# Four GNN layers on one core: the end of each batch paced to 117 units instead of 75

## The chip, the cores and the metric

One core of a Trainium2 chip. The time is that of the device for one execution, in microseconds, the median of several runs.

## The reference, cut to what matters

Sixteen graphs of 1024 nodes and 128 features go through four layers. Each layer adds its output to its input. Layers 0 and 1 multiply by the dense adjacency, layer 2 scores every edge with a small network (twice, each time with an update of the nodes), layer 3 is graph attention:

```python
# layer 0, 1: x = x + gnn(relu(layernorm(x)), adj)      (dense adj)
# layer 2, for l in 0, 1:
#   scores = sigmoid(relu(a[:, :, None] + b[:, None]) @ We2[l])   per edge
#   messages = (adjacency * scores) @ x ; x = layernorm(x + mlp([x, messages]))
# layer 3:
e = (Wh1 + swapaxes(Wh2)) * (A + eye); e = where(e >= 0, e, 0.2 * e)
attention = softmax(where(A_ > 0, e, NEG_INF)); h_prime = attention @ Wh
x = x + elu(h_prime)
```

## The kernel before

Only about 1.5% of the adjacency is set, so the kernel turns each block of it into one-hot tiles (`on`, `onT`, `om`, `omT`: the building) and runs the edge scores on the edges alone (the rounds). Three lanes are emitted side by side in each period: the rounds of batch b, the end of batch b-1 (last update and layer 3) and the beginning of batch b+1 (layers 0 and 1, then the building). Each lane yields a number of units a step, and the lane that is least far through its allowance goes next:

```python
MAIN_US, FIRST_US, LAST_US = 243.0, 118.0, 75.0      # allowances
...
        def weave(self, lanes):
            out_of = [[0.0, i, gen, us] for i, (gen, us) in enumerate(lanes)]
            while out_of:
                least = min(out_of, key=lambda v: v[:2])
                us = next(least[2], None)
                if us is None:
                    out_of.remove(least)
                else:
                    least[0] += us / least[3]
```

Emission is a priority, not the final order: when the program is built, the instructions are put in order for each engine, and an instruction that is believed ready can pass another. The strips of layer 3 look like this (cut):

```python
N_ROW = {"m": 2, "a": 2, "c": 1}          # row buffers; strips use "c": one buffer
...
            for lo, hi in L3_ROWS:         # three blocks of 3, 3 and 2 tiles
                for k in range(0, T, 2):   # four strips each: 12 a batch
                    at = strip(k, lo, hi)  # DMA into the one buffer
                    ...                    # e = (wh1 + wh2) * at         VectorE, twice
                    nc.vector.scalar_tensor_tensor(e, e, L3_ALPHA, e, op0=OP.mult, op1=OP.max)
                    nc.scalar.activation(e, e, AF.Exp)
                    nc.vector.scalar_tensor_tensor(e, at, 0.0, e, op0=OP.is_gt, op1=OP.mult)
                    ...                    # matmuls hp; the mask above is the last reader of at
                    yield 1.2 * n
```

## Time and profile before

| | before |
|---|---|
| time | 5532 us |
| a period (mean of 12, from the first `hid` of a batch to that of the next) | 337.1 us |
| of it until the first `rank` of the building (stretch A) / from there on (stretch B) | 189.5 / 147.6 us |
| store of the output, after the period's first `hid` | 309 us |
| VectorE waiting for a strip | 2.0 us a period |
| TensorE clock at half | 2.0 us a period |

A `hid` is an instruction of the rounds and a `rank` one of the building; rows two to four come from the starts of single instructions in the trace.

The other readings of before are in the prediction.

### The profile page before, as it was taken

The page shows a single profiled execution, that of the slowest core. Times are in us where ns is not written, and L with a number is a line of the kernel's source. Part 1 is how long each engine was busy: PE and PEld are TensorE (multiplying, and loading weights), DVE is VectorE, ACT ScalarE, POOL GpSimd, SP SyncE. Part 2 cuts the span into 40 slices and gives each one's busy share as a digit, 9 for nine tenths or more (in the row PEclk, how much of TensorE's full clock was granted, in tenths as well). Part 3 has the DMA queues.
Part 4 walks back from the last instruction along what each step waited for, and adds up shares of the span by engine and source line. Part 5 has one row for each costly group of instructions (what it writes and reads, how often), then busy time and mean ns, then how long its engine had stood idle before and what let it go on. Part 6 is the DMA issues. An engine that isn't in the chain of part 4 may idle for free.

```text
span 5526.6 us, 113576 instructions
## 1 busy us (share of the span) xinstructions
PE 5037.3 (91%) x45109; PEld 3719.3 (67%) x45109; DVE 4304.6 (78%) x10759; ACT 3054.6 (55%) x6790; POOL 184.9 (3%) x137
## 2 busy tenths in 40 slices
PE   5999999999999999999999999999999999999996
PEld 4676766667676666666766666676766767666664
DVE  4777787878879787787877878778787887978886
ACT  4555564655647555465555646556465564655543
POOL 0000000000000000000000000000000000000000
PEclk8999999999999999999999999999999999999998
DMA  6242424243242433424334142432424324243111
GB/s 174 62 136 87 121 68 137 76 125 101 84 140 66 125 96 92 131 66 120 98 102 124 56 139 81 122 106 71 140 72 128 97 85 133 67 124 95 54 63 51
DMA packets 740139, 554.56 MB, mean 100 GB/s; under 512 B 32272, under 2 KB 686352, under 8 KB 739600
## 3 DMA queue, kind: packets, MB, share of 16 engines
q1 hardware_dynamic: 734496, 545.58, 33.6%
q8 instruction: 356, 5.83, 0.4%
q10 hardware_dynamic: 5104, 1.65, 0.1%
q14 instruction: 183, 1.50, 0.1%
HBM read 446.44 MB, written 100.66 MB: 99 GB/s over the span
## 4 chain that ended last, share of the span: by engine, by line
PE 47%; DVE 27%; DMA 9%; ACT 9%; issue 4%; POOL 3%; SPq 0%; ACTq 0%; DVEq 0%; POOLq 0%
PE pre L986 11%; DVE val L1075 10%; PE p L1097 6%; DMA at<-in_adj_dram 4%; DVE hid L1003 4%; PE nb L288 4%; PE msg L1114 4%; PE bb L296 3%; PE sc L1018 3%; DMA a<-adjT 2%; DVE omT L854 2%; PE hp L505 2%; POOL st L243 2%; PE h L342 2%; PE tn L743 2%
## 5 line engine op out<-in xcount | busy, mean ns | idle before, releaser
L1003 DVE SCALAR_TENSOR_TENSOR hid<-pre,hid 128x320 f16<-128x320 f32 (+1 forms) x2048 | 993.0, 504 | 294.9 <-ACT hid L1002 283.9
L1002 ACT ACTIVATE hid<-pre 128x320 f16<-128x320 f32 (+1 forms) x2048 | 900.7, 454 | 501.3 <-PE pre L986 473.4
L986 PEld LDWEIGHTS <-part 128*128 128x128 f16 x8192 | 753.4, 98 | 450.5 <-issue 236.2
L986 PE MATMUL pre<-on,part 128*128 128x320 fp8e4 (+1 forms) x4096 | 966.2, 309 | 71.6 <-DVE hid L1003 60.6
L986 PE MATMUL pre<-om,part 128*128 128x320 fp8e4 (+1 forms) x4096 | 994.3, 309 | 0.0
L1114 PE MATMUL msg<-upd,xf 128*128 128x128 f32 (+3 forms) x3008 | 613.6, 323 | 2.2 <-DVE upd L1105 2.2
L1075 DVE TENSOR_TENSOR val<-onT,u 128x384 f32<-128x384 fp8e4 (+1 forms) x1152 | 607.8, 580 | 4.0
L1097 PE MATMUL p<-val,omT 128*128 128x128 f16 x6528 | 534.2, 219 | 29.8 <-DVE val L1075 27.7
L1097 PEld LDWEIGHTS <-omT 128*128 128x128 fp8e4 x6528 | 436.7, 96 | 84.4 <-DVE val L1075 34.4
L1075 DVE TENSOR_TENSOR val<-omT,u 128x384 f32<-128x384 fp8e4 x896 | 439.2, 549 | 0.0
L861 ACT ACTIVATE om<-pm 128x320 fp8e4<-128x320 f32 (+1 forms) x576 | 268.9, 467 | 294.4 <-PE pm L817 285.8
L1114 PEld LDWEIGHTS msg<-upd,xf 128*128 128x128 f32 x3008 | 414.2, 191 | 25.6 <-DVE upd L1105 13.9
L1105 DVE SCALAR_TENSOR_TENSOR upd<-p,adj 128x512 f32<-128x512 f32 x512 | 348.5, 681 | 82.4 <-PE p L1097 82.2
L1097 PE MATMUL p<-val,onT 128*128 128x128 f16 x4480 | 374.1, 219 | 1.4 <-DVE upd L1105 1.4
L847 ACT ACTIVATE onT<-pn 128x384 fp8e4<-128x384 f32 (+1 forms) x576 | 297.6, 517 | 102.7 <-PE pn L817 82.8
L1039 ACT ACTIVATE srow<-sc,be_s,down 128x128 f32<-128x128 f32 (+2 forms) x512 | 259.7, 540 | 168.2 <-PE sc L1018 166.9
L505 PE MATMUL hp<-wh,e 128*128 128x129 f32 x2048 | 318.3, 285 | 22.3 <-DVE e L502 22.3
L1097 PEld LDWEIGHTS <-onT 128*128 128x128 fp8e4 x4480 | 304.6, 97 | 36.9 <-issue 8.8
L505 PEld LDWEIGHTS hp<-wh,e 128*128 128x128 f32 x2048 | 275.5, 195 | 51.9 <-DVE e L502 29.6
L804 ACT ACTIVATE far<-iota_off,mid 128x384 f16<-128x384 f16 x448 | 269.5, 625 | 39.9 <-DVE on L808 34.3
L288 PE MATMUL nb<-z,ct 128*128 128x128 f32 x2048 | 279.3, 282 | 12.4 <-DMA ct<-in_adj_dram 11.9
L1018 PE MATMUL sc<-hid,slide 128*32 128x320 f16 (+1 forms) x4096 | 268.3, 315 | 18.2 <-DVE hid L1003 15.7
(220 smaller groups left out, 8106.8 us busy)
## 6 DMA issues: line engine op xcount, KB each, us to landing
at<-in_adj_dram SPq DMA_DIRECT2D x128, 512.0 KB, 4.3
ct<-in_adj_dram SPq DMA_DIRECT2D x128, 512.0 KB, 4.6
adjT<-tn SPq DMA_DIRECT2D x128, 512.0 KB, 5.1
l<-adjT SPq DMA_DIRECT2D x128, 512.0 KB, 4.2
adj<-adjT SPq DMA_DIRECT2D x256, 256.0 KB, 3.4
a<-adjT SPq DMA_DIRECT2D x128, 384.0 KB, 3.5
adj<-adjT SPq DMA_DIRECT2D x448, 64.0 KB, 2.1
adj<-adjT SPq DMA_DIRECT2D x192, 128.0 KB, 2.6
```

The costliest lines, as they stand in the source:

```text
L288: nc.tensor.matmul(ps, mat[:, k], z[:, k], start=(k == 0), stop=(k == T - 1))
L505: nc.tensor.matmul(sums[:, t], e[:, i, t * P : (t + 1) * P], wh[:, k + i, : D + 1], start=False, stop=True, skip_group_check=True,)
L804: nc.scalar.activation(far[:, : ck * P], self.iota[t == u][:, : ck * P], AF.Abs, bias=s.mid[:, i : i + 1])
L847: nc.scalar.activation(onT, pn[:, : ck * P], AF.Copy, saturate=False)
L986: nc.tensor.matmul(pre[:, :c], path.parts[node // Q][:, k, node % Q, v], hot[:, :c], start=(hot is on and k == 0), stop=(hot is om and k = ...
L1002: nc.scalar.activation(hid[:, 0, :c], pre[:, :c], AF.Relu)
L1003: nc.vector.scalar_tensor_tensor(hid[:, 1, :c], pre[:, :c], 0.0, hid[:, 0, :c], op0=OP.max, op1=OP.subtract)
L1018: ins = nc.tensor.matmul(self.sc[g * G : (g + 1) * G, : self.c], self.path.slide[:, self.l, G - 1 - r : 2 * G - 1 - r], self.hid[self.done ...
L1075: nc.vector.tensor_tensor(pair[:, i % 2, :ck], right[:, :ck], v.to_broadcast([P, ck, P]), op=OP.mult)
L1097: nc.tensor.matmul(self.ps[d][:, i], left[:, k], halves[:, k, :, h], start=(k, h) == terms[0], stop=(k, h) == terms[-1],)
L1105: nc.vector.scalar_tensor_tensor(upd, self.ps[d], S_SCALE, self.adj[:, d * Q : (d + 1) * Q], op0=OP.add, op1=OP.mult,)
L1114: nc.tensor.matmul(self.msg[h][:, (lo - h * Q) * P : (hi - h * Q) * P], self.xf[mb // Q][:, mb % Q], up, start=False, stop=True, skip_grou ...
```

## The change

Its intent: the building is heavy on VectorE, and the end of the batch before lies partly beside it. With a larger allowance the end counts as less far along at each step, so it is emitted sooner, and is done when the building begins.

```diff
 MORE_DIAG = 0
 
 
+
 MAIN_US = 243.0
 FIRST_US = 118.0
-LAST_US = 75.0
+LAST_US = 117.0
```

The added blank line shifts line numbers by one: L496 of before is L497 after.

## The prediction

> **What bounds the kernel now.** I read the page first, then the kernel's interleaving code, then busy time by stretch of one batch, the groups of instructions inside a stretch, and the waits.
>
> ```profile
> PE 5037.3 (91%) x45109; PEld 3719.3 (67%) x45109; DVE 4304.6 (78%) x10759; ACT 3054.6 (55%) x6790; POOL 184.9 (3%) x137
> ...
> PE 47%; DVE 27%; DMA 9%; ACT 9%; issue 4%; POOL 3%; SPq 0%; ACTq 0%; DVEq 0%; POOLq 0%
> ```
>
> The first line is busy time by engine, the second the chain that ended last. TensorE leads both, but VectorE holds 27% of the chain: an average over stages with different limits. The interleaving code says which stages. In each period three lanes are emitted together, each step going to the lane that is least far through its own allowance: the rounds of batch b (steps add up to about 243.6 units, allowance 243), the end of batch b-1 (last update 20 units, last layer 12 plus 38.4 for twelve strips, 70.4 in all, allowance 75) and the beginning of batch b+1 (70 units of layers 0 and 1, then 46.8 units of building the one-hot tiles, 116.8, allowance 118). So the building starts at 70/118 = 0.59 of the way and lasts to the end; the end of the batch before reaches 70.4/75 = 0.94 and lies beside both.
>
> In the trace, batch starts (the first `hid` of each batch) are 335 to 340 us apart. I take the period 1480 to 1815 us, in which the first `rank` of the building is at 1669. Busy time by stretch: before and during the building, then the last period, which has rounds and end but no beginning of another batch.
>
> ```profile
> 1480.00:1669.00 189.00, 175.68 (x1470) 130.38 (x1469) 137.04 (x373) 93.11 (x203) 9.81 (x7) 1.00 0.45 130
> 1669.00:1815.00 146.00, 135.85 (x1350) 99.82 (x1350) 130.82 (x298) 97.07 (x223) 1.64 (x1) 1.00 0.22 68
> 5184.00:5434.00 250.00, 226.11 (x1897) 154.93 (x1897) 203.96 (x480) 102.51 (x232) 6.10 (x5) 0.98 0.19 57
> 1669.00:1753.00 84.00, 79.53 (x826) 59.89 (x826) 80.65 (x183) 59.29 (x139) 0.00 (x0) 1.00 0.22 66
> ```
>
> Columns: stretch, length, busy PE, PEld, DVE, ACT, POOL, then granted clock and DMA. VectorE is busy 137/189 = 73% in the first stretch (call it A) and 131/146 = 90% in the second (B); in the first 84 us of B it is 80.65/84 = 96%[...]. ScalarE goes from 49% to 66%. TensorE shows 93% in both, but that needs correcting:
>
> ```profile
> 2057.66 0.33 PE L850 MATMUL pq<-rank,on 128*128 128x128 f16 x3
> ...
> 2059.62 0.22 PE L1097 MATMUL p<-val,omT 128*128 128x128 f16 x1
> ```
>
> One matmul of 128 columns shows 0.22 us, three in a row 0.33: each further one costs 0.055, and the rest is a tail that overlaps the next. Giving every matmul the start-to-start time that its own form shows when matmuls run in a row (0.055 us for 128 columns of f16, 0.135 for 320, 0.11 for 128 of f32) TensorE needs 158.6 us in A (84%) and 115.9 in B (79%). So B is held by VectorE and A by TensorE and its bubbles: the building waits there for `omT`, `on`, `onT` in turn.
>
> **What the Trainium skill says.** "Perfetto Trace Analysis", Identifying the Most-Contended Engine: matmul occupancy doesn't measure distance from the limit, occupancy of VectorE and ScalarE does; the two timeline lines above agree. The same page, Optimization Strategy: where the most contended engine changes over time, interleaving the regimes may help. That is what this change attempts: VectorE goes from 73% to 90% between A and B. "PSUM — Partial Sum Buffer", Engine vs sequencer instructions: VectorE and ScalarE queues are strict FIFO. So an instruction of the end that stands ahead of one of the building delays it; the 96% agrees with a queue that rarely runs dry, though no line proves the order.
>
> **The change part by part.** One number, the allowance of the end, goes from 75 to 117 (and a blank line moves all line numbers by one). No instruction is added, removed or resized. With 117 the end reaches 70.4/117 = 0.60 when it is done: just where the building begins (0.59). What moves is that part of the end which lies in B now:
>
> ```profile
> L505 PE MATMUL hp<-wh,e 128*128 128x129 f32 x80 | 12.9, 284 | 0.2 <-DVE e L502 0.2
> ...
> L496 DVE SCALAR_TENSOR_TENSOR e<-whr,whc,a 128x256 f32<-128x256 f32 (+1 forms) x14 | 7.3, 532 | 0.5 <-DMA a<-adjT 0.5
> L502 DVE SCALAR_TENSOR_TENSOR e<-a,e 128x768 f32<-128x768 f32 (+1 forms) x8 | 6.5, 813 | 0.0
> L500 DVE SCALAR_TENSOR_TENSOR e<-e 128x512 f32<-128x512 f32 (+1 forms) x7 | 5.6, 795 | 0.0
> L501 ACT ACTIVATE e<-e 128x512 f32<-128x512 f32 (+1 forms) x7 | 5.1, 726 | 0.0
> L495 DVE TENSOR_TENSOR a<-a,ident 128x128 f32<-128x128 f32 x7 | 1.8, 284 | 0.0
> L513 ACT ACTIVATE o<-hp,rsum 128x128 f32<-128x128 f32 x5 | 1.6, 366 | 0.1
> L425 DVE SCALAR_TENSOR_TENSOR o<-o,neg 128x1024 f32<-128x1024 f32 x1 | 1.2, 1216 | 0.0
> L426 DVE SCALAR_TENSOR_TENSOR xb<-o,xb 128x1024 f32<-128x1024 f32 x1 | 1.2, 1214 | 0.0
> L424 ACT ACTIVATE neg<-neg 128x1024 f32<-128x1024 f32 x1 | 1.1, 1057 | 0.1
> ```
>
> These are groups inside B: count, busy us, mean ns, idle before. VectorE: 7.3 + 6.5 + 5.6 + 1.8 + 1.2 + 1.2 + 0.7 (`neg`) + 0.5 (sums) = 25 us. ScalarE: 5.1 + 1.6 + 1.1 = 8 us. TensorE: 80 matmuls at 0.112 paced = 9 us. After the move:
>
> - B: VectorE 131 - 25 = 106, TensorE 116 - 9 = 107, ScalarE 97 - 8 = 89 us.
> - A: VectorE 137 + 25 = 162, TensorE 159 + 9 = 168, ScalarE 93 + 8 = 101 us.
>
> In B nothing is then near 90% at the old length. How short it gets depends on how well three nearly equal engines overlap. The last period shows what two lanes with equal loads manage: VectorE 204/250 = 82%, TensorE paced 197/250 = 79%. I take 83% for TensorE and VectorE in B, which has the building's independent tiles as filler: 107/0.83 = 129 us, 17 less than 146. In A, TensorE keeps its 84%: 168/0.84 = 200 us, 11 more than 189; VectorE there is then at 162/200 = 81%, as in the last period. I let the end's independent strips fill some of A's bubbles (`hid`, `xf`, the load of `xm`) and count 8 to 9 instead of 11. Net: -17 + 8.5 = -8.5 us for each period that has all three lanes. Those are b = 1 to 14: 14 x -8.5 = -119 us. The first period has no end lane, the last no building (its end just moves forward, 0 ± 3 us), and the drain is unchanged. 5532 - 119 gives about 5413; I put down 5412.
>
> **The rivals.**
>
> 1. *The gain is given back in A.* TensorE's total work is the same; A already waits for chains. If A pays in proportion at a worse packing (168/0.81 = 207 us, +18), the net is about 0 and the time stays at 5530. For it: A's TensorE reaches 84% with VectorE at 73%, and each extra wait for `hid` or `val` there costs both. Against it: in stretches of A TensorE is nearly solid, so A can be packed.
>
> 2. *The strips' loads block the one DMA queue.* All strips go through one row buffer, and the queue waits in order:
>
> ```profile
> SPq L1190 <- DVE e L502: 579.7, 108, 38.1
> SPq L689 <- PE tn L743: 792.9, 107, 26.1
> ```
>
> This is SyncE's own waiting in the whole run: 580 us for a strip's buffer, 38 at most. In the change twelve strips must pass in about (0.60 - 0.27) x 335 = 110 us, one each 9 us, where a cycle of load (3.3 us median from issue to landing), three VectorE passes, Exp and the release takes 8 us unhindered (3.3 + 0.6 + 1.2 + 0.9 + 0.8 + 0.9). Loads of `at`, `ct` and the rounds' rows wait behind it, in the very stretch whose DMA share is 0.45. Then A grows by some 20 us and the kernel is about 1% slower, 5570. Against it: the end runs late rather than blocks if other work is placed ahead of a strip that isn't ready.
>
> 3. *B packs as its start does now.* If VectorE and TensorE reach 90% in B (119 us, -27) and A pays 6, the net is -21 a period, 5240. For it: VectorE's 96% now. Against it: equal loads on three engines hinder one another more than one full engine does.
>
> 4. *The order on the engines isn't the emission order.* Of the last layer's strips, 7 of 12 lie in B, by work 53%, where the units say 67%: the order is adjusted when the program is built, so some of the move has happened already. I counted from the trace, so it's in the sum, but a reordering can undo part of the rest.
>
> **Range and chances.** Rival 1 and the central case are the nearest, 3 and 2 the ends. Half-way to 3 gives 5300, part of 2 gives 5520. I expect it to hold 5300 to 5510 eight times in ten. The line for 2% faster is 5532.2 x 0.98 = 5421.6, just above my centre: 0.53 for faster, 0.43 within, 0.04 slower.
>
> **What would show it.** In the changed profile the period should be 326 to 331 us. The output's store, now 307 to 312 us after the batch's first `hid`, should come at about 200 to 220. VectorE in the building stretch should fall from 90% to 80 to 85% and that stretch to about 129 us; the stretch before should grow to about 198 us with VectorE over 80%. The waits of TensorE for `omT` should shrink. The prediction is wrong if the building stretch stays near 146 us with VectorE idle (then chains bound it, not VectorE), if the stretch before grows by 15 us or more, or if waits for strips or `at` loads grow by several us a period.

## More of the kernel before

Every run of the kernel before lay between 5515 and 5543 us.

The waits, from the list of who waited for whom (total us, times, longest):

```profile
DVE e L496 <- DMA a<-adjT: 31.9, 37, 3.1
DVE a L495 <- DMA a<-adjT: 4.3, 4, 2.5
```

So VectorE waits hardly at all for strips: 36 us in the whole run.

## The result, and the profile after

The changed kernel took 5735 us (5728 to 5736, four runs) against 5534 in the same sessions. The ratio is 1.036, with a 95% interval of 1.034 to 1.038: 3.6% slower, where 2.2% faster was predicted and 5510 was the upper end of the range. Ratios here are the mean time of one kernel's fast runs over that of the other's of the same rounds, so not quite the ratio of the medians quoted.

The page of the changed kernel, busy time by engine and the chain that ended last:

```profile
PE 5137.8 (90%) x45109; PEld 3783.2 (66%) x45109; DVE 4323.8 (75%) x10759; ACT 3072.7 (54%) x6790; POOL 176.8 (3%) x137
...
PE 41%; DVE 34%; DMA 10%; ACT 8%; POOL 3%; issue 3%; SPq 0%; ACTq 0%; DVEq 0%; POOLq 0%
```

The counts are the same to the instruction, VectorE's work hardly grew (4305 to 4324 us), and yet its share of the chain rose from 27 to 34%: it now holds others up more often. TensorE's busy time rose by 100 us for the same matmuls.

A period grew from 337.1 to 351.0 us (mean of 12). Busy time by stretch of one period, then the last period:

```profile
1527.00:1735.00 208.00, 187.92 (x1542) 141.00 (x1541) 153.94 (x404) 98.03 (x211) 9.31 (x7) 0.98 0.44 130
1735.00:1878.00 143.00, 129.76 (x1284) 93.15 (x1283) 115.57 (x267) 93.20 (x215) 1.64 (x1) 0.99 0.18 53
5379.00:5641.00 262.00, 226.50 (x1878) 154.29 (x1877) 204.70 (x479) 103.77 (x231) 5.66 (x5) 0.97 0.18 54
```

The columns are those of the prediction: stretch, length, PE, PEld, DVE, ACT, POOL, clock, DMA. Stretch A grew from 189 to 208 us, B shrank from 146 to 143, and the last period grew from 250 to 262. In A VectorE has 17 us more work but a share of 74% only (153.94/208): the time isn't VectorE's work. The clock column went from 1.00, 1.00 and 0.98 to 0.98, 0.99 and 0.97.

Who waits for strips now (the same view as in the section on before):

```profile
DVE e L497 <- DMA a<-adjT: 84.3, 43, 3.7
DVE a L496 <- DMA a<-adjT: 61.2, 45, 3.3
```

That makes 145 us of VectorE standing still, 36 before; over the twelve periods 9.5 us each against 2.0. VectorE in order of time, in one period (start, length, engine, line, operation, tiles, count, and in brackets the idle time before it and its releaser), then SyncE's queue in the same stretch:

```profile
2722.22 0.95 DVE L503 SCALAR_TENSOR_TENSOR e<-a,e 128x768 f32<-128x768 f32 x1
...
2727.53 0.62 DVE L497 SCALAR_TENSOR_TENSOR e<-whr,whc,a 128x384 f32<-128x384 f32 x1 [3.50 <-DMA a<-adjT]
...
2730.91 0.96 DVE L503 SCALAR_TENSOR_TENSOR e<-a,e 128x768 f32<-128x768 f32 x1 [0.91 <-ACT e L502]
2731.78 0.34 DVE L330 SCALAR_TENSOR_TENSOR o<-nb,deg,b_bc 128x128 f32<-128x128 f32 x1
2732.04 1.21 DVE L1004 SCALAR_TENSOR_TENSOR hid<-pre,hid 128x480 f16<-128x480 f32 x2
2735.97 0.49 DVE L496 TENSOR_TENSOR a<-a,ident 128x128 f32<-128x128 f32 x2 [2.72 <-DMA a<-adjT]
```

```profile
2723.20 0.37 SPq L1191 DMA_DIRECT2D a<-adjT  x1
...
2731.89 0.36 SPq L1191 DMA_DIRECT2D a<-adjT  x1
...
2741.18 0.36 SPq L1191 DMA_DIRECT2D a<-adjT  x1
```

The mask of one strip (L503) ends at 2723.17; 0.03 us later the load of the next strip into the same buffer starts; 4.3 us later the strip's first pass can run. By the in-order queue that the prediction cites, that pass stands at the head of VectorE's queue, and the engine idles 3.50 us. TensorE did not stand still meanwhile: it ran `hp`, `h` and `nb`. The next loads follow after 8.7 and 9.3 us: the pace at which strips are due now, with nothing to spare. In the kernel before, three successive loads in the building stretch were 12.9 and 16.7 us apart.

TensorE in order of time shows another loss:

```profile
2699.69 0.83 PE L1098 MATMUL p<-val,omT 128*128 128x128 f16 x10
2702.34 0.43 PE L987 MATMUL pre<-on,part 128*128 128x320 fp8e4 x2 [1.82 <-DVE hid L1004]
...
2703.79 0.47 PE L987 MATMUL pre<-om,part 128*128 128x320 fp8e4 x1
```

```profile
2703.79 0.74 PE L987 MATMUL pre<-om,part 128*128 128x320 fp8e4 x2
```

(The last line is from a later start of the same view.) TensorE stands still for 1.82 us. No strip is to blame here: it waits for a `hid` (L1004) that stood behind eight `val` passes of VectorE (2698.06 to 2701.88). At 2703.5 the granted clock drops to half for 3.4 us, and a second matmul of 320 columns adds 0.74 - 0.47 = 0.27 us, where at full clock it adds 0.43 - 0.30 = 0.13. In the changed kernel half-clock pieces come back in most periods at nearly the same places, about 74, 126, 170, 200 and 238 us after its start: 19.3 us a period at half clock, 2.0 before. Gaps of TensorE over 1.5 us number 4.5 a period, 1.7 before. Adding up the matmuls that ran in half-clock pieces, each at its full-clock spacing, gives 8.5 us of work that took twice as long, 1.0 before: 7.5 us a period lost.

So beside the 13.9 us a period stand 7.5 us more of VectorE waiting for strips and 7.5 us lost at half clock. That their sum is near the loss proves nothing, and in time the two hardly meet. Of the 9.5 us of strip waits only 0.3 fall into time in which TensorE is idle (by the modelled ends of its matmuls), and of the 53 drops of the clock in the twelve periods one has a strip wait in the 5 us before it. If the waits cost time, they do it later, through work that VectorE finishes late; no line shows that path whole. The experiments had to show which is a cause.

### The profile page after: what moved, and what is told of

Read it like the earlier page. It is cut to its first block, busy times and chain, and to the rows that moved or that the text cites.

```text
span 5733.9 us, 113669 instructions
## 1 busy us (share of the span) xinstructions
PE 5137.8 (90%) x45109; PEld 3783.2 (66%) x45109; DVE 4323.8 (75%) x10759; ACT 3072.7 (54%) x6790; POOL 176.8 (3%) x137
## 4 chain that ended last, share of the span: by engine, by line
PE 41%; DVE 34%; DMA 10%; ACT 8%; POOL 3%; issue 3%; SPq 0%; ACTq 0%; DVEq 0%; POOLq 0%
DVE val L1076 13%; PE pre L987 11%; PE p L1098 4%; DMA a<-adjT 4%; DVE hid L1004 4%; DMA at<-in_adj_dram 4%; PE msg L1115 3%; PE bb L297 3%; PE sc L1019 3%; PE h L343 2%; PE nb L289 2%; DVE omT L855 2%; DVE e L497 2%; POOL st L244 2%; PE hp L506 2%
## 5 line engine op out<-in xcount | busy, mean ns | idle before, releaser
L1004 DVE SCALAR_TENSOR_TENSOR hid<-pre,hid 128x320 f16<-128x320 f32 (+1 forms) x2048 | 1002.4, 505 | 282.6 <-ACT hid L1003 269.7
L987 PE MATMUL pre<-on,part 128*128 128x320 fp8e4 (+1 forms) x4096 | 980.2, 313 | 132.3 <-DVE hid L1004 121.6
L1098 PE MATMUL p<-val,omT 128*128 128x128 f16 x6528 | 517.5, 219 | 30.4 <-DVE val L1076 25.8
L1098 PE MATMUL p<-val,onT 128*128 128x128 f16 x4480 | 402.7, 222 | 5.1 <-DVE upd L1106 5.1
L1098 PEld LDWEIGHTS <-onT 128*128 128x128 fp8e4 x4480 | 319.4, 98 | 56.0 <-issue 15.7
L506 PE MATMUL hp<-wh,e 128*128 128x129 f32 x2048 | 291.3, 290 | 25.5 <-DVE e L503 24.9
L855 DVE TENSOR_TENSOR omT<-pq,odd_off 128x384 fp8e4<-128x384 f32 x448 | 247.7, 553 | 86.6 <-PE pq L851 84.0
L818 PE MATMUL pm<-eye,omT 128*128 128x128 f16 x1856 | 203.4, 223 | 106.9 <-DVE omT L855 95.9
L497 DVE SCALAR_TENSOR_TENSOR e<-whr,whc,a 128x384 f32<-128x384 f32 (+1 forms) x384 | 208.2, 567 | 117.9 <-DMA a<-adjT 84.3
```

The lines of the kernel that those rows point to most:

```text
L497: nc.vector.scalar_tensor_tensor(e[:, i], wh1[:, lo * P : hi * P], wh2[:, k + i : k + i + 1], at[:, i], op0=OP.add, op1=OP.mult,)
L506: nc.tensor.matmul(sums[:, t], e[:, i, t * P : (t + 1) * P], wh[:, k + i, : D + 1], start=False, stop=True, skip_group_check=True,)
L855: nc.vector.tensor_tensor(omT.rearrange("p (k m) -> p k m", m=P), pq[:, :ck], self.odd[t == u][:, :, None].to_broadcast([P, ck, P]), op=OP ...
L987: nc.tensor.matmul(pre[:, :c], path.parts[node // Q][:, k, node % Q, v], hot[:, :c], start=(hot is on and k == 0), stop=(hot is om and k = ...
L1004: nc.vector.scalar_tensor_tensor(hid[:, 1, :c], pre[:, :c], 0.0, hid[:, 0, :c], op0=OP.max, op1=OP.subtract)
L1098: nc.tensor.matmul(self.ps[d][:, i], left[:, k], halves[:, k, :, h], start=(k, h) == terms[0], stop=(k, h) == terms[-1],)
```

## The experiments

The theories were:

- **Strip loads.** One buffer for strips that are now due each 9 us puts waits at the head of VectorE's queue.
- **One-bank chain.** The building stretch did not shrink since the building goes through one PSUM bank, not since VectorE holds it.
- **Crowding.** Anything of the end that moves into the first stretch delays the rounds there.
- **Order.** Any edit gives a new order on the engines, and some orders are simply worse.

All kernels, with median time, ratio to before, and per period (mean of 12) the length, VectorE's waits for strips and the matmul work done at half clock. "2 buffers" implies MORE_OFF 2, explained below.

| run | allowance, edit | us | ratio | period | strip waits | half-clock work |
|---|---|---|---|---|---|---|
| before | 75 | 5532 | | 337.1 | 2.0 | 1.0 |
| after | 117 | 5735 | 1.036 | 351.0 | 9.5 | 8.5 |
| last90 | 90 | 5571 | 1.007 | 339.2 | 5.7 | 3.8 |
| last113 | 113 | 5627 | 1.018 | 343.5 | 6.3 | 4.3 |
| early_upd | last update early, layer 3 spread | 5572 | 1.007 | 339.9 | 0.9 | 5.6 |
| bank2 | 117, second bank for the building | 5675 | 1.027 | 346.1 | 9.9 | 6.7 |
| moff2_75 | 75, MORE_OFF 2 | 5500 | 0.995 | 335.2 | 1.4 | 0.8 |
| moff2_113 | 113, MORE_OFF 2 | 5592 | 1.011 | 340.1 | 6.6 | 3.8 |
| moff2 | 117, MORE_OFF 2 | 5674 | 1.026 | 347.2 | 9.4 | 9.3 |
| moff2_121 | 121, MORE_OFF 2 | 5611 | 1.014 | 341.5 | 7.3 | 5.8 |
| row2_75 | 75, 2 buffers | 5472 | 0.990 | 333.0 | 0.7 | 2.4 |
| row2_90 | 90, 2 buffers | 5482 | 0.992 | 333.4 | 1.0 | 3.1 |
| row2_113 | 113, 2 buffers | 5426 | 0.981 | 328.3 | 3.0 | 0.4 |
| row2 | 117, 2 buffers | 5503 | 0.995 | 334.6 | 3.2 | 4.2 |
| row2_121 | 121, 2 buffers | 5484 | 0.992 | 333.5 | 1.4 | 6.5 |
| row2_bank | row2 with bank2 | 5592 | 1.011 | 341.2 | 3.4 | 6.2 |
| k1_75 | 75, half strips, 2 half buffers | 5502 | 0.995 | 335.6 | 2.1 | 2.2 |
| k1_117 | 117, half strips, 2 half buffers | 5624 | 1.017 | 341.5 | 4.8 | 3.8 |
| light_75 | 75, two strip passes left out | 5383 | 0.974 | 328.0 | 1.2 | 1.4 |
| nohp_75 | 75, three of four hp left out | 5451 | 0.986 | 331.4 | 2.1 | 2.1 |

The last two give a wrong result; all others were correct.

### How far forward, and a second buffer

```diff
-LAST_US = 117.0
+LAST_US = 90.0      # last90
```

> The change with an allowance of 90 instead of 117: the end of a batch is done at 70.4/90 = 0.78 of the way. If the loss grows evenly with how far the end is drawn forward, (0.94-0.78)/(0.94-0.60) = 47% of the 201 us: about 5628 us. If crowding only hurts once the whole last layer lies before the building[...], nearer to 5560 us. If the strips' loads were the only cause, little loss as well, since a strip would be due each 13 us or so.

It lost 41 us, 20% of the change's loss for 47% of the way. The loss is not proportional, and the strips' waits already show.

For the second buffer the on-chip memory was full: with two full row buffers the build failed, 4 KiB a partition short. So the buffers were cut to what a strip needs, and two spare one-hot tiles of each kind were given up. The prologue, which borrowed that buffer, does with four row buffers instead of five.

```diff
-N_ROW = {"m": 2, "a": 2, "c": 1}
+N_ROW = {"m": 2, "a": 2, "c": 2}
-MORE_OFF = 4
+MORE_OFF = 2
-            return self.work.tile([P, T, P], F32, tag=f"row{v}", ...)
+            return self.work.tile([P, 6 if v == "c" else T, P], F32, tag=f"row{v}", ...)
             self.alone(self.a, "amcam")
+            self.rows_of["a"] = "amam"
```

> The change with two row buffers for the strips of the last layer instead of one (buffers of 6 blocks instead of 8, and MORE_OFF 2 instead of 4 to make room, which moff2 tries alone). Theory 'strip loads': VectorE's waits for a<-adjT (145 us in all after, 36 before) hold the queue and with it hid and TensorE; they should nearly vanish and the time fall by 80 to 145 us to 5590 to 5650. Theory 'crowding of the in-order queues': the waits go but the time stays within 30 us of 5735.

The control has MORE_OFF 2 alone:

> Control for row2: the change with MORE_OFF 2 instead of 4 (two spare one-hot tiles of each kind fewer) and nothing else. Both theories: 5735 us within 25 us; if the building needs the spares it is slower by more, and row2 has to be read against this.

The control fell by 60 us, more than expected of it, so row2 has to be read against it: 5674 to 5503, 172 us less, with waits for strips down from 9.4 to 3.2 us a period. The strip theory had named the direction; the effect was larger than its forecast. The gain is in the periods (347.2 to 334.6 us), not in the prologue, which the edit also touches. The same at other allowances:

> The kernel before (allowance 75) with row2's two strip buffers and MORE_OFF 2: what the change is worth once the strips no longer wait. If the second buffer only repairs what the change broke, 5525 to 5550 us, like before, and the change gains 25 to 45 us with it (row2 was 5502). If the second buffer helps any spread, this is at or below 5500 and the change is then worth nothing or less.

> Two strip buffers, MORE_OFF 2, allowance 90 (the end done at 0.78 of the way). If the gain of drawing the end forward grows with the distance, between row2_75 and row2's 5502; if there is a best place in between because the loads of the beginning lie in the first 0.59, below both, 5470 to 5495.

Both lie below row2: with two buffers the end drawn forward was 30 us slower here, not faster. The missing corner of the square, the kernel before with MORE_OFF 2:

> Control: the kernel before with MORE_OFF 2 and nothing else; the missing corner of the square of strip buffers (1, 2) and allowances (75, 117). If moff2's 60 us under the change is a chance of the order on the engines, anything within 60 us of 5530. If fewer spares help as such, about 5470, and row2_75's gain is then not the second buffer's; if 5525 to 5540, the second buffer gains some 60 us even at 75.

At 5500 us it lies within the 60 us of chance, and between the other two cases named. The square at MORE_OFF 2 is then: one buffer 5500 to 5674 (+174), two buffers 5472 to 5503 (+31).

### How large is chance?

```diff
-LAST_US = 117.0
+LAST_US = 113.0      # last113
```

> The change with 113 instead of 117: as good as the same pace, another draw of the order on the engines. By the strip theory 5715 to 5735 us. If two kernels of nearly the same pacing differ by 50 us or more, that is the size of chance by which all single comparisons here have to be read.

It differs from the change by 107 us and misses the strip theory's 5715 to 5735. A pace 3% apart is the same idea, so single comparisons between differently built kernels are uncertain by some tens of us up to a hundred, although each kernel repeats its own time within 30. Two more draws a side were therefore taken:

> Two strip buffers, allowance 113. Strip theory: 5480 to 5550 us, near row2's 5502. If row2 was a lucky order: 5580 us or more.

> Two strip buffers, allowance 121. Strip theory: 5490 to 5560 us. If row2 was a lucky order: 5580 us or more.

> One strip buffer, allowance 113, MORE_OFF 2: 5610 to 5690 us by the strip theory (5674 at 117). Under 5570 would mean that one buffer is no steady cost at this pace.

> One strip buffer, allowance 121, MORE_OFF 2: 5640 to 5730 us by the strip theory, a little above 113. Under 5570 as for moff2_113.

One buffer at 113, 117, 121: 5592, 5674, 5611, mean 5626. Two buffers: 5426, 5503, 5484, mean 5471. All of one side lie 89 us or more above all of the other, and the mean difference is 155 us. moff2_113 and moff2_121 came in a little below what was expected of them, row2_113 and row2_121 too. The second buffer's gain is thus hardly chance: three against three fall apart like this by luck once in 20, and at each allowance the pair differs by 126 to 172 us. It also says what the change is worth with most of the wait gone: mean 5471 against 5472 for the kernel with two buffers at 75, that is nothing, give or take the 76 us that the three draws spread.

Where the gain lies settles more than the totals do. Means of twelve periods, stretches A and B:

| allowance | A, 1 buffer | A, 2 buffers | B, 1 buffer | B, 2 buffers |
|---|---|---|---|---|
| 75 | 191.0 | 192.2 | 144.2 | 140.8 |
| 113 | 205.1 | 197.1 | 135.1 | 131.2 |
| 117 | 210.9 | 196.5 | 136.3 | 138.1 |
| 121 | 209.5 | 199.1 | 132.0 | 134.4 |

At 113 to 121 the second buffer shortens A by 10.9 us in the mean (208.5 to 197.6) and B not at all (134.5 and 134.6). At 75, where strips are rarely late, it does nothing for A. In the chain that ended last the loads of strips take 191, 258 and 225 us of the whole run with one buffer, and 134, 19 and 39 with two. So the one buffer costs time in A, where the strips now lie. One period of moff2_113, to be held against row2_113 further below:

```profile
1834.00:2041.00 207.00, 188.46 (x1555) 142.18 (x1554) 155.10 (x407) 99.76 (x215) 9.65 (x7) 0.98 0.44 129
2041.00:2176.00 135.00, 125.30 (x1266) 90.35 (x1265) 114.22 (x264) 91.28 (x211) 1.64 (x1) 1.00 0.20 58
```

Another way to two buffers, with the change's own memory and MORE_OFF: strips of one block row instead of two, in two buffers of half the size.

```diff
-                for k in range(0, T, 2):
+                for k in range(T):
-                    yield 1.2 * n
+                    yield 0.6 * n
-                    for i in range(2):
+                    for i in range(1):
-            return self.work.tile([P, T, P], ...
+            return self.work.tile([P, 4 if v == "c" else T, P], ...   # "c": 2 of these
```

> The change with strips of one block row instead of two in two buffers of half the size: same memory, MORE_OFF 4. It has 12 more of each of two VectorE passes and of Exp a period, an estimated 1.5 to 3 us of VectorE and 2 to 3 of ScalarE. Theory 'strip loads': waits for a<-adjT fall from 9.5 to under 4 us a period and the time to 5500 to 5600 us. Rival 'row2 was a lucky order': waits may fall, but the time stays at 5630 to 5740, the range of the one-buffer kernels at 113 to 117.

> The same halved strips at allowance 75: 5480 to 5560 us (before is 5530, row2_75 5472; the smaller instructions cost some). With k1_117 it gives the effect of drawing the end forward without the wait for strips a second time: 30 us by row2, so -30 to +90 here, against 201 (or 174) with one buffer.

This is a weak result. The waits were halved to 4.8 us, not removed. The loss against k1_75 was 122 us instead of 201, outside the forecast of -30 to +90. k1_117 missed the strip theory's range by 24 us and its rival's by 6, and it equals last113, which has one buffer (5627). Half strips mean loads twice as often and half as much cover for each, which may be why; it supports the theory in direction at most.

### Moving the last update alone

```diff
-            yield from lane.layer3(xt, strip, self.zero, f"{b}")
+            for us in lane.layer3(xt, strip, self.zero, f"{b}"):
+                yield us * 1.783
```

> One strip buffer as in the change; only the last update (first 20 units) is drawn forward, the last layer is then spread until 0.94 of the way as before (its units times 1.783, the allowance stays 117). Theory 'strip loads': a strip is due each 21 us at least, no waits for strips (2 us a period), half-clock time a few us a period: 5515 to 5555 us. Theory 'anything of the end drawn into the first stretch delays the rounds': 20/70 of the 201 us or more on top, 5590 us and over.

It took 5572 us, between the two theories. The strips wait only 0.9 us a period, as expected. But 5.6 us of matmul work ran at half clock, 4.6 more than before, while the period is only 2.8 longer. So strips are not the only way to half-clock pieces. Given the size of chance, 40 us from one kernel is no cost shown.

### What holds the building stretch?

```diff
-                    lanes.append((self.last(done, b - 1), LAST_US))
+                    lanes.append((self.ending(done, b - 1), LAST_US))
+        def ending(self, s, b):
+            yield from self.last(s, b)
+            self.a.banks = [self.own["c"], self.own["a"]]
```

> The change, and once the end of a batch is all emitted its PSUM bank (c) is lent to the building lane, which has one bank (a) in both kernels. Theory 'one-bank chain': the building stretch is held by the round trips pn, onT, pq, omT, pm, om through one bank (about 3.4 us for each of 36 tiles = 122 us, in both kernels), which is why taking 25 us of VectorE work out of it saved only 5 us; with two banks it should shrink from 143 to 105 to 120 us, the whole to about 5250 to 5420 us. Rival 'TensorE or VectorE holds that stretch': no gain, 5700 to 5735 us.

> row2 with bank2's lent PSUM bank. bank2 took 60 us off the change and shortened the building only from 123 to 114 us a period, so theory 'one-bank chain' explains at most part. If the two gains are independent: 5440 to 5470 us. If the lent bank's gain was only another draw of the order on the engines (as moff2's 60 us must be), 5490 to 5530.

The one-bank chain fell, though neither run met any of its forecasts. The building itself went from 123 to 114 us (first to last `rank`), but stretch B only from 143 to 140; the 60 us are no more than chance gives, and added to row2 the same edit cost 89 us. Then VectorE's and TensorE's work was taken out directly, from the kernel before:

```diff
-                    nc.vector.scalar_tensor_tensor(e, e, L3_ALPHA, e, op0=OP.mult, op1=OP.max)
                     nc.scalar.activation(e, e, AF.Exp)
-                    nc.vector.scalar_tensor_tensor(e, at, 0.0, e, op0=OP.is_gt, op1=OP.mult)   # light_75
```

> Wrong result on purpose: the kernel before without the leaky slope and the mask of the strips (two of the three large VectorE passes), 20.8 us less VectorE work a period, about 12 of it in the building stretch. If VectorE holds that stretch, as predicted, it shortens by about 12 us a period, and the whole by 170 us or more. If not (the same time then hardly cared for VectorE's 90%), it shortens by under 5 us and the whole by under 80.

```diff
-                    for i in range(2):
+                    for i in range(2 if k == 0 else 0):
                         for t in range(n):
                             nc.tensor.matmul(...)      # hp
-                nc.vector.tensor_copy(rsum[:, 0, lo:hi], sums[:, :, D])
+                nc.vector.tensor_scalar(rsum[:, 0, lo:hi], sums[:, :, D], 1.0, None, op0=OP.add)   # nohp_75
```

> Wrong result on purpose: the kernel before with one in four pairs of the strips' matmuls hp (96 of 128 a period left out, about 10.7 us of paced TensorE work, 6.7 of it in the building stretch; one is added to the sums so that none is zero). If TensorE's own work in its order is what both stretches are made of, the period falls by 8 to 11 us, the whole by 110 to 160. If VectorE holds the building stretch, only the part in the stretch before counts, 4 us a period, 60 us.

(The wording of the last is loose: one in four is kept, 96 of 128 left out.)

light_75, busy time in one period before and from the first `rank`:

```profile
1781.00:1971.00 190.00, 177.47 (x1468) 131.23 (x1467) 129.35 (x364) 91.21 (x199) 9.17 (x7) 0.99 0.45 130
1971.00:2109.00 138.00, 133.99 (x1357) 99.82 (x1355) 120.13 (x284) 97.88 (x226) 1.64 (x1) 1.00 0.23 71
```

With some 8 us of VectorE work gone from A, A stayed at 190 us: VectorE's load isn't what holds it. With 12 us of passes gone from B, B went from 147.6 to 138.3 in the mean, 9 us: there it is VectorE for the most part, as far as one built order shows. The whole gained 149 us, between the two forecasts (170 and more, under 80). nohp_75 shortened A by 1.1 and B by 4.6 us for 10.7 us of TensorE work in all, 5.7 of a period, also between its forecasts, so TensorE's own work is only partly on the path. The predicted reading of the two stretches was right for B.

## Why the prediction was wrong, point by point

Two terms of the sum failed: B was to give 17 us a period and gave 4, and A was to cost 8.5 and cost 18. With the sign of each, -8.5 became +13.9. The cause of A's part is shown, that of B's only in part.

**What bounds the kernel.** Right for B (light_75), half right for A: TensorE with its bubbles, and light_75 shows that VectorE's load there is not the limit.

**What moves.** 25 us of VectorE work and 9 of TensorE were to leave B. In the changed kernel TensorE's paced work is 166.5 and 108.4 us in A and B, 168 and 107 predicted. VectorE's is 153.9 and 115.6, 162 and 106 predicted. Of the 10 us too much in B some 6 are there because the end ran late: its output came 221 us after the first `hid`, 13 us into the building, with one strip and the closing passes left for B. The rest comes from the reckoning: it took the durations of single groups from a busy time in which consecutive passes overlap (durations in B of the kernel before add up to 150 us, its busy time is 131). In row2 no strip lies in B and VectorE still has 115.0 us there.

**B packs at 83% and gives 17 us.** This term failed, and by size it is the larger error. B gave 4 us (147.6 to 143.3, means). VectorE's share is 115.6/143 = 81%, much as assumed, but its load there was 10 us larger: 115.6/0.83 is 139 us. TensorE's paced share is only 76%. The strip buffer is not the cause, since B is the same with one and two (134.5 us at MORE_OFF 2). Why B is still 4 us longer than 139, and why it is 5 to 7 us shorter with MORE_OFF 2 at 113 and 117 (140.6 to 135.1, 143.3 to 136.3), stays open. The two half-clock pieces at about 200 and 238 us lie around its beginning.

**A keeps TensorE's 84% and costs 8 to 11 us.** This is the error whose cause is shown, in the term that I took over from the old A. A's paced share fell to 166.5/208 = 80%, and A cost 18 us (189.5 to 207.7), as rival 1 had put it for a packing of 81%. With the second strip buffer A is 197.6 us in the mean, the forecast 198: so the 84% about holds once the buffer is doubled. Rival 2 named the buffer, the growth of A by some 20 us, the pace of 9 us and the cycle of some 8 us, and the measured cycle was 8.7 to 9.3. But it sought the harm in SyncE's queue, which in fact waited less for strips than before (308 us for the mask L503, 580 before for L502), and it was waved away with "the end runs late rather than blocks if other work is placed ahead of a strip that isn't ready". It did both: other work was not ahead, and VectorE stood 2.7 to 3.5 us for a strip's first pass. I had cited the in-order queue for the wrong victim.

**The clock.** Nothing in the prediction allowed for it; the page shows a lower clock only in the first and last slice. In the twelve periods of the changed kernel, 42 of the 54 gaps of TensorE over 1.5 us were followed by a drop of the clock within 3.6 us, and only 1 of 53 gaps from 1.2 to 1.5 us. But in the kernel before it was 5 of 20 gaps over 1.5 us, and 11 of the 53 drops after, and 25 of row2's 27, came without such a gap. So no length of a single gap decides it here. Over the eighteen correct kernels of the table a least-squares line puts the period at 330.5 us + 1.03 for each us of strip waits + 0.90 for each us of half-clock work; it explains 78% of the variance. That is a description, not an experiment. No run changed the clock alone, so how much of the loss the half clock causes stays open.

**The last period, 0 ± 3 us.** It grew by 12 (250 to 262).

**Rival 4, the order.** Mentioned, and far too small: moff2 and last113 show 60 and 107 us.

What would the central case have looked like? row2_113, the change with 113 and two strip buffers, by stretch:

```profile
1789.00:1985.00 196.00, 184.27 (x1560) 139.85 (x1559) 154.93 (x411) 98.20 (x213) 10.05 (x7) 1.00 0.47 137
1985.00:2117.00 132.00, 123.97 (x1269) 90.01 (x1266) 114.38 (x261) 92.45 (x216) 1.64 (x1) 1.00 0.20 58
```

A 196 and B 132 us, full clock: close to the 198 and 129 that were forecast, and 5426 us, 1.9% faster than before and the best correct kernel found. But its neighbours at 117 and 121 took 5503 and 5484, and two buffers without any drawing forward 5472, so the advantage over 5472 cannot be told from a lucky order. What the runs show as steady is the second strip buffer where the end is drawn forward: 155 us, all of it in A. Even with it, drawing the end forward gives B's 6 us (140.8 to 134.6) for A's 5 (192.2 to 197.6).

## What to carry to other kernels

Before drawing work forward, take the longest chain through its smallest buffer (here release, load, three passes) and divide the new time by the number of turns. Here a chain of some 8 us met turns of 9: VectorE stood still 9.5 us a period, and its share of busy time in A, 74%, did not show it. Look at the stretch where the buffer is used, not at the total alone: that is where the second buffer's 10.9 us were found. Then look at the granted clock, here 19.3 us a period at half. And try a neighbouring value before believing a few per cent: here 113 for 117 moved the time by 107 us.

## What the Trainium skill lacked or had wrong

- "TensorE: Matmul & The Clock Gate", HAM oscillation: its rule is no idle gaps of TensorE beyond about 3.4 us. Here the rule was kept and was not enough: in the twelve periods of the changed kernel the longest gap was 2.5 us, and the clock still dropped to half 53 times, 19.3 us a period in all. The page's next section does name frequent short idles as a cause, without a length; the runs show no single length either (counts under "The clock").
- The same page, Back-to-back issue gap, gives about 81 ns a matmul as the sustained pace of weight load and matmul pairs at N=128. Here matmuls of 128 f16 columns, each with its own fp8 weights (`p<-val,omT` and `p<-val,onT`), started 58 ns apart in the median (the ten in the line above: (0.83 - 0.22)/9 = 0.068 us each).
- "Perfetto Trace Analysis", Optimization Strategy, says that interleaving regimes may help where the contended engine changes. It names too few buffers only as a cause of consistent bubbles, and lacks the warning that the moved work's own buffer must stand the new pace: with one strip buffer the mean was 5626 us, with two 5471.
- No page that I read says how large the chance of the built order is: 60 and 107 us of 5600 for edits that should be nearly neutral.
